# Reduced-precision passes for the ±1 convolutions, and expert rows scattered to token order

## The chip, the cores and the metric

The kernel runs on one core of a Trainium2 chip. A core has a matrix engine (TensorE, PE in the profile, with its weight loads as PEld), three engines for the rest (VectorE or DVE, ScalarE or ACT, GpSimd or POOL), a queue engine that mostly issues transfers (SyncE or SP), and 16 DMA engines that move data between the memory of the chip (DRAM tiles) and the core's own memory. Every engine works through its own list of instructions in order and waits on semaphores for the others. The metric is the device time of one execution in microseconds; runs of one kernel lie within some 0.2% of each other here.

## The reference, cut to what matters

The input `x` is (4, 256, 48, 48) in FP32: four images with 256 channels and 2304 tokens (pixels). Two layers follow each other; what is computed in FP32 there has to be met closely, because routing decisions hang on it.

- Layer 0: a 7x7 convolution with dilation 2 gives attention weights over 49 taps, and the attention is added to `x`. Then a router picks the 1151 tokens of each image with the largest weight, and these alone go through an FFN (256 to 1024 to 256).
- Layer 1, convolution: the normalised image is convolved with four kernels of 64 outputs each, two horizontal and two vertical of 5 taps, dilation 1 and 2. Their weights are binarised, `where(w < 0, -1, 1)`, so each product is the input or its negative. The four results side by side are again 256 channels and are added to `x`.
- Layer 1, experts: each token's norm is multiplied with gate weights for 8 experts; softmax gives a probability and the first expert with the largest one. Tokens take slots of their expert in token order, 1440 at most. Each expert is an FFN (256 to 1024 to 256, ReLU); its result is multiplied by the gate's probability, infinities and NaN are replaced, and it is added to the token's row. A token without a slot keeps its row.

The output is the image with channels in front.

## The kernel before, in words

*First stage (to about 2020 us).* Layer 0's convolution and attention, image by image. Beside it zeros are written into `xbuf`, the buffer of 11520 expert slots in DRAM, 40 writes of 292.5 KB on the SP queue, since slots that stay empty must hold numbers.

*Second stage (to 3020 us).* First seven FFNs of layer 0, on 384 rows each, beside the rank counts of the last image. Then a loop of 24 steps (`for s in ...`, from L640), one for each group of 384 tokens (8 image rows), with five more FFNs in every second of its first steps. It is a software pipeline written out by hand: what depends on other engines is issued a step later, so that five groups are under way at once. In one step stand, in this order of issue:
 - `load`: a group's rows from DRAM into `xt3`, a tile that keeps the residual stream of every token on the core to the end, and their channel norm. `token_norm` (L105 to L111) is statistics on VectorE (L107, L108), an addition and a power on GpSimd (L109, L110, tile `bnrs`), and the final scaling on VectorE (L111). It is called three times for a group.
 - `to_channels`: transposes on TensorE (`pn`, L511), and a copy of each half into the padded image `xq` (L513), one by ScalarE and one by VectorE.
 - `conv1`: 7 offsets x 2 halves of the channels x 2 (horizontal and vertical) = 28 FP32 products of 384 columns on shifted views of `xq` (L524, `pc`); the weights `cw` hold 1, -1, and 0 where one of a pair has no tap. ScalarE adds the bias into `cv` (L528).
 - `to_tokens`: transposes back (`pcv`, L539), the addition to the residual in `xt3` (L541), and the second norm into `row` (3 buffers), whose columns past the channels are set to zero by GpSimd (L535).
 - `gate`: transposes (`pl`), the gate product (`pgate`), softmax and choice of expert in a dozen small VectorE operations; the probability is put into `row` as column 256.
 - `place`: running counts give each token's slot; `gslot` and `kept` keep slot and mark for the end, `si` (L616) is the slot as an integer, too large for a token that finds no place. Three indirect writes from GpSimd (L618) scatter `row` (260 numbers a token) into `xbuf`. Writes to one DRAM tile wait for each other.

*Third stage (to 3701 us).* 24 passes, three for each expert, of 480 slots. `gather` (a plain read) brings the slots' rows as `xe` (three buffers), asked for a pass ahead; transposes; two products (`peh` L702, `pey` L710); VectorE adds a bias (L712), multiplies by the probability (L713) and repairs what isn't finite (L721 to L724); a plain write stores the result in `ybuf` (L725), by slot.

*Last stage (to 3814 us).* For each of the 72 tiles of 128 tokens GpSimd gathers the rows by slot (`yt`, L757), VectorE multiplies by `kept` and adds `xt3` (L760), TensorE transposes (`po`, L763), ScalarE and VectorE copy to `o`, and SP writes the output (L767).

Of the kernel before, what the change touches and what calls it, by code (L numbers as in the profile page):

```python
# [8 lines left out]
F32 = mybir.dt.float32  # L9
I32 = mybir.dt.int32  # L10
# [6 lines left out]
P = 128  # L17
B, C, H, W = 4, 256, 48, 48
HW = H * W  # 2304 tokens of an image
NT = HW // P  # 18 tiles of 128 tokens  # L20
NG = 6  # groups of 8 image rows
GT = 384  # tokens of a group
KA = 49  # attention taps
SELK = 1151  # tokens that layer 0's FFN processes: top_k's first k - 1
NSEL = 9  # tiles of 128 ranks that hold them
E, CAP = 8, 1440  # experts, and the slots of each
FF = 1024
NF = FF // P
XROW = 260  # a row of the experts' buffer: 256 channels, the gate, padding
HOFF = [-4, -2, -1, 0, 1, 2, 4]  # offsets of layer 1's convolutions  # L30
FMAX = 3.4028234663852886e38

# One image, by row and column parity, is four 24x24 images in which the 7x7
# convolution and the attention have no dilation. They are padded to 30x30.
SP = 30
SRC = 10 * SP  # source pixels of four output rows
PITCH = 306  # a row of the attention matrix in DRAM; skewed writes use PITCH + 1
# [3 lines left out]
def metaformer_kernel(ctx: ExitStack, tc: tile.TileContext, i, out):  # L41
# [18 lines left out]
    # before[p, j] = j < p; after[p, j] = j > p; upto[p, j] = p <= j  # L60
# [13 lines left out]
    # 1 for every rank but the last of the ninth tile  # L74
# [3 lines left out]
    ids = const.tile([P, NT], I32, tag="ids", name="ids")  # L78
    nc.gpsimd.iota(ids, pattern=[[P, NT]], base=0, channel_multiplier=1)

# [14 lines left out]
    # rows of layer 0: [x + LN(x) | LN(x)], by image  # L95
    xl = [dram.tile([HW, 2 * C], F32, tag=f"xl{b}", name=f"xl{b}") for b in range(B)]
    # token of each rank, by image
    order = [dram.tile([HW, 1], I32, tag=f"order{b}", name=f"order{b}") for b in range(B)]
    xbuf = dram.tile([E * CAP, XROW], F32, tag="xbuf", name="xbuf")
    ybuf = dram.tile([E * CAP, C], F32, tag="ybuf", name="ybuf")  # L100

    def token_norm(work, src, dst, eps, np_=P):
        """dst = LN(src) over the free dim of [np_, 256]."""
# [9 lines left out]
    # Ranks of an image's router weights, ties by the lower token, are counted three tiles at  # L113
    # a time beside the next image's convolution.
# [4 lines left out]
    # the first tile has no earlier tokens, the last no later ones  # L119
# [3 lines left out]
    def rank_rows(b, ps):  # L123
        """An image's router weights along the free dim of every partition."""
        w = w_img[b]
        nc.vector.tensor_scalar_add(w, w, br)
        for k0 in range(0, NT, 4):
            n = min(4, NT - k0)
            pt = ps.tile([P, 4, P], F32, tag="t", name=f"pw{b}_{k0}")
            for k in range(n):  # L130
                nc.tensor.transpose(
                    pt[:, k], w[:, k0 + k:k0 + k + 1].to_broadcast([P, P]), ident)
            nc.scalar.copy(wrow[:, k0 * P:(k0 + n) * P],
                           pt[:, :n].rearrange("p k t -> p (k t)"))

    def rank_count(b, j):
        """Tokens that come before each token of tiles 3j..3j+2."""
# [21 lines left out]
    # ======================================================================  # L159
    # Layer 0: dynamic 7x7 attention, and the ranks of its tokens  # L160
    # ======================================================================
    with ExitStack() as s1:
# [28 lines left out]
        # batch norm as k2 * inv + shift  # L191
# [12 lines left out]
        # normalised image, channels by parity image; its padding stays zero  # L204
        xp = wpool.tile([P, 2, 4, SP, SP], F32, tag="xp", name="xp")
        nc.vector.memset(xp.rearrange("p c q r x -> p (c q r x)"), 0.0)
        # the last six columns of each row of 30 stay zero
        k1s = [wpool.tile([P, 4, 4, SP], F32, tag=f"k1{n}", name=f"k1{n}") for n in range(2)]
        # attention rows spread over the sources' pitch; what is no tap stays zero
# [7 lines left out]
        # empty slots of the experts hold zeros  # L217
        zero = wpool.tile([P, 585], F32, tag="zero", name="zero")
        nc.gpsimd.memset(zero, 0.0)
        zrows = xbuf.rearrange("n r -> (n r)").rearrange("(k p r) -> k p r", p=P, r=585)  # L220
# [3 lines left out]
        def norm_a(b, j):  # L224
            """Subtract the channel means of 8 image rows; start the variance."""
# [32 lines left out]
        def conv(b, g):  # L258
            """Convolution of output rows 4g..4g+3 of the four parity images."""
# [11 lines left out]
        def sources(b, g):  # L271
            """Sources with pixels on partitions, four padded rows at a time."""
# [17 lines left out]
        def attend(b, g):  # L290
            """Softmax over the taps, laid out as a matrix [target, source]."""
# [27 lines left out]
        def mix(b, g):  # L319
            """x += attention; then tokens, their norm, and their router weights."""  # L320
# [40 lines left out]
        for s in range(B * NG + 1):  # L361
# [5 lines left out]
            # rows that the next image's group takes are no longer read  # L367
# [14 lines left out]
            for k in range(2 * s, min(2 * s + 2, 40)):  # L382
                nc.sync.dma_start(zrows[k], zero)

    # tokens of the residual stream from here to the end, by image
    xpool = pool("xtok", 1)
    xt3 = [xpool.tile([P, NT, C], F32, tag=f"xt3_{b}", name=f"xt3_{b}") for b in range(B)]
    gslot = [xpool.tile([P, NT], I32, tag=f"gslot{b}", name=f"gslot{b}") for b in range(B)]
    kept = [xpool.tile([P, NT], F32, tag=f"kept{b}", name=f"kept{b}") for b in range(B)]

    # ======================================================================
    # Layer 0's FFN on the selected tokens; layer 1's convolutions and routing
    # ======================================================================
    with ExitStack() as s2:
# [14 lines left out]
        # The horizontal pair, then the vertical: each is one convolution with 128 outputs  # L409
        # over the offsets of both, with zeros where one of them has no tap.  # L410
        cws = []
        for n in range(2):
            cw = wpool.tile([P, 2, 7, P], F32, tag=f"cw{n}", name=f"cw{n}")
            nc.gpsimd.memset(cw.rearrange("p c t o -> p (c t o)"), 0.0)
# [19 lines left out]
        # E - e, so that the first of equal experts is the largest  # L434
# [3 lines left out]
        # tokens that each expert has so far, in every partition  # L438
        taken = wpool.tile([P, E], F32, tag="taken", name="taken")
        nc.gpsimd.memset(taken, 0.0)  # L440
        # normalised image, padded by 4; its padding stays zero
        xq = wpool.tile([P, 2, H + 8, W + 8], F32, tag="xq", name="xq")
        nc.gpsimd.memset(xq.rearrange("p c r x -> p (c r x)"), 0.0)

        def fetch(b, h):
            """Rows of 384 ranks."""
# [12 lines left out]
        def ffn(b, h, idx2, g):  # L459
            """x + LN(x) + w * FFN(LN(x)), back to the tokens' rows."""  # L460
# [36 lines left out]
        def load(b, g):  # L497
            """8 rows of layer 1's input, and their channels' norm."""
            x = xt3[b][:, 3 * g:3 * g + 3]
# [5 lines left out]
            return xn  # L505

        def to_channels(b, g, xn):
            for cc in range(2):
                pt = ps_t.tile([P, GT], F32, tag="t", name=f"pn{b}_{g}_{cc}")
                for k in range(3):  # L510
                    nc.tensor.transpose(pt[:, k * P:(k + 1) * P],  # L511
                                        xn[:, k, cc * P:(cc + 1) * P], ident)
                (nc.vector.tensor_copy if cc else nc.scalar.copy)(  # L513
                    xq[:, cc, 4 + 8 * g:12 + 8 * g, 4:4 + W],
                    pt.rearrange("p (r x) -> p r x", x=W))

        def conv1(b, g):
            cv = work.tile([P, 2, GT], F32, tag="cv", name=f"cv{b}_{g}")
            for n in range(2):
                ps = ps_m.tile([P, GT], F32, tag="m", name=f"pc{b}_{g}_{n}")  # L520
                for t, d in enumerate(HOFF):
                    dy, dx = (d, 0) if n else (0, d)
                    for cc in range(2):
                        nc.tensor.matmul(  # L524
                            ps, lhsT=cws[n][:, cc, t],
                            rhs=xq[:, cc, 4 + 8 * g + dy:12 + 8 * g + dy, 4 + dx:4 + dx + W],
# [286 lines left out]
```

## Time and profile before

The time is 3820.05 us, the median of three runs (3817.47 to 3824.94). The profiled execution has a span of 3814.3 us.

| stage | from to (us) | span | TensorE busy |
|---|---|---|---|
| first two convolution steps | 2284.9 to 2323.2 | 38.3 | 37.9 |
| steps with five FFNs among them | 2323.2 to 2620.8 | 297.6 | 289.1 |
| thirteen plain steps | 2620.8 to 2955.6 | 334.8 | 325.4 |
| drain of the routing | 2955.6 to 3019.7 | 64.1 | 16.9 |
| experts | 3019.7 to 3700.7 | 681.0 | 668.4 |
| last stage | 3700.7 to 3814.3 | 113.6 | 50.8 |

Line numbers (L524) are those of the kernel printed above. In a line of groups the fields are: line, engine, operation, output<-inputs by the names of the tiles, shape, count (x), then busy microseconds, nanoseconds of one, and the idle time of the engine just before, with what ended it. An FP32 product leaves two weight loads and two matrix records. In a line of a stage the fields are the window, its length, the busy time of each engine in the order PE, PEld, DVE, ACT, POOL with the number of its records, then TensorE's granted clock as a share of the full one, the busy share of the DMA engines and the GB/s that they moved. In a line of waits the waiting engine, tile and line come first, then whom it waited for, then microseconds in total, number of times and the longest. A line of the timeline has start, duration, engine, line, operation and, in brackets, how long the engine was idle before it and what released it. Waits of an engine that is not the bottleneck cost nothing.

### The profile page before, as it was taken

How to read it: one execution, taken by the hardware profiler on the slowest of the kernel's cores; microseconds unless marked ns; L12 is line 12 of the kernel's file. 1: busy time of each engine (PE TensorE's matmuls, PEld its weight loads, DVE VectorE, ACT ScalarE, POOL GpSimd, SP SyncE). 2: the span in 40 equal slices, each digit the busy share in tenths (PEclk: the TensorE clock that was granted, in tenths of full speed). 3: DMA queues.
4: the chain of work that ended last, by engine and by line, in shares of the span. 5: the costliest groups of instructions: out<-in, count | busy, mean ns of one | idle time of the engine just before them, and what ended most of it. 6: DMA issues, size and time to landing. Idle time of an engine off the chain costs nothing. (4 is left out here: it accounts for less than half of the span.)

```text
span 3814.3 us, 32485 instructions
## 1 busy us (share of the span) xinstructions
PE 3545.5 (93%) x12832; PEld 2248.8 (59%) x12832; DVE 1211.3 (32%) x3618; ACT 434.0 (11%) x779; POOL 480.0 (13%) x774
## 2 busy tenths in 40 slices
PE   6999999999999999999994789999999499999985
PEld 3566666666666666666663556666565366666652
DVE  3012124312235112261116312333443243333434
ACT  1001000000100000100001111211010022121211
POOL 1000001100001000020002322232332100000006
PEclk9999999999999999999996889999999699999995
DMA  7001100001100000110002221111000222222106
GB/s 231 13 25 39 36 25 25 25 25 35 40 25 25 25 25 27 34 27 21 21 21 76 62 63 31 41 34 44 18 17 18 80 61 59 59 62 66 49 27 193
DMA packets 122840, 174.36 MB, mean 46 GB/s; under 512 B 17089, under 2 KB 96193, under 8 KB 122689
## 3 DMA queue, kind: packets, MB, share of 16 engines
q1 hardware_dynamic: 92800, 111.41, 10.4%
q0 software_dynamic: 13824, 33.23, 2.9%
q10 hardware_dynamic: 16064, 27.66, 2.2%
q8 instruction: 100, 1.64, 0.2%
q14 instruction: 52, 0.42, 0.0%
HBM read 91.69 MB, written 80.58 MB: 45 GB/s over the span
## 5 line engine op out<-in xcount | busy, mean ns | idle before, releaser
L264 PE MATMUL c<-xp,cw 128*128 128x384 f32 x4704 | 1568.5, 492 | 0.9 <-DVE xp L256 0.9
L264 PEld LDWEIGHTS c<-xp,cw 128*128 128x128 f32 x4704 | 885.0, 189 | 663.0 <-issue 304.1
L524 PE MATMUL pc<-xq,cw 128*128 128x384 f32 x1344 | 467.1, 501 | 0.0
L329 DVE COPY av<-pa 120x192 f32<-120x192 f32 x96 | 32.0, 358 | 1096.9 <-PE pa L327 1096.9
L524 PEld LDWEIGHTS pc<-xq,cw 128*128 128x128 f32 x1344 | 254.8, 195 | 164.6 <-issue 12.8
L710 PE MATMUL pey<-ew,ehid 128*120 128x256 f32 x1536 | 335.4, 379 | 0.0
L702 PE MATMUL peh<-xeT,ew 128*128 128x480 f32 x768 | 316.5, 571 | 3.1 <-ACT xeT L697 3.1
L710 PEld LDWEIGHTS pey<-ew,ehid 128*120 128x120 f32 x1536 | 281.1, 183 | 59.2 <-issue 10.4
L109 POOL TENSOR_SCALAR bnrs<-bnmv 128x1 f32<-128x1 f32 x216 | 47.1, 223 | 1865.3 <-DVE bnmv L108 1864.0
L702 PEld LDWEIGHTS peh<-xeT,ew 128*128 128x128 f32 x768 | 145.0, 191 | 159.7 <-issue 151.0
L337 PE MATMUL pv<-av,xt 120*128 120x96 f32 (+1 forms) x1152 | 226.6, 329 | 0.0
L337 PEld LDWEIGHTS pv<-av,xt 120*128 120x128 f32 (+1 forms) x1152 | 181.8, 214 | 39.3 <-issue 11.4
L712 DVE TENSOR_TENSOR ey<-pey,eb 120x256 f32<-120x256 f32 x96 | 40.7, 424 | 431.1 <-PE pey L710 431.1
L269 ACT ACTIVATE k<-c,cb 128x384 f32<-128x384 f32 x24 | 14.0, 583 | 1323.4 <-PE c L264 1266.1
L757 POOL DMA_INDIRECT yt<-ybuf,gslot x72 | 69.9, 971 | 720.8 <-DMA ybuf<-ey 699.1
L704 ACT ACTIVATE ehid<-peh,eb 128x480 f32<-128x480 f32 x192 | 127.0, 662 | 294.6 <-PE peh L702 293.2
L480 PE MATMUL ph<-gt,fw 128*128 128x384 f32 x384 | 137.8, 520 | 6.2 <-ACT gt L475 5.8
L486 PE MATMUL py<-fw,hid 128*128 128x256 f32 x576 | 126.8, 379 | 3.0 <-DVE y L489 3.0
L110 POOL TENSOR_TENSOR bnrs<-bnrs,mhalf 128x1 f32<-128x1 f32 x216 | 125.0, 583 | 13.3
L486 PEld LDWEIGHTS py<-fw,hid 128*128 128x128 f32 x576 | 109.3, 190 | 21.1 <-DVE y L489 3.8
L480 PEld LDWEIGHTS ph<-gt,fw 128*128 128x128 f32 x384 | 76.7, 203 | 63.6 <-ACT gt L475 9.5
L763 PE MATMUL po<-ident,yt 128*128 128x128 f32 x144 | 50.8, 448 | 57.2 <-DVE yt L760 56.1
(169 smaller groups left out, 2599.3 us busy)
## 6 DMA issues: line engine op xcount, KB each, us to landing
xl<-rows SPq DMA_DIRECT2D x24, 768.0 KB, 3.5
ew<-in_L_ffn_w_dram ACTq DMA_DIRECT2D x16, 1024.0 KB, 5.4
skew<-sp SPq DMA_DIRECT2D x24, 575.6 KB, 4.3
at<-skew SPq DMA_DIRECT2D x24, 562.5 KB, 4.8
xbuf<-zero SPq DMA_DIRECT2D x40, 292.5 KB, 7.8
xe<-xbuf SPq DMA_DIRECT2D x24, 487.5 KB, 4.5
ybuf<-ey SPq DMA_DIRECT2D x24, 480.0 KB, 3.6
x<-in_x_dram SPq DMA_DIRECT2D x24, 384.0 KB, 3.4
```

The source lines that it names most:

```text
L109: nc.gpsimd.tensor_scalar_add(rs[:np_], mv[:np_, 1:2], eps)
L110: nc.gpsimd.tensor_tensor(rs[:np_], rs[:np_], mhalf[:np_, 0:1], ALU.pow)
L264: nc.tensor.matmul(ps, lhsT=cw1[:, cc, t, :], rhs=xp[:, cc, :, 4 * g + ki:4 * g + ki + 4, kj:kj + 24], start=(t == 0 and cc == 0), stop=(t ...
L337: nc.tensor.matmul(pv[:, q], lhsT=xts[b, g + k][:n, q, cc * P:(cc + 1) * P], rhs=av[:n, q, k], start=(k == 0), stop=(k == 2))
L480: nc.tensor.matmul(ph, lhsT=fw1[:, cc, f * P:(f + 1) * P], rhs=gt[:, cc], start=(cc == 0), stop=(cc == 1))
L486: nc.tensor.matmul(py, lhsT=hid[:, f, k * P:(k + 1) * P], rhs=fw2[:, f], start=(f == 0), stop=(f == NF - 1))
L524: nc.tensor.matmul(ps, lhsT=cws[n][:, cc, t], rhs=xq[:, cc, 4 + 8 * g + dy:12 + 8 * g + dy, 4 + dx:4 + dx + W], start=(t == 0 and cc == 0) ...
L702: nc.tensor.matmul(ph, lhsT=w1[:, cc, f * P:(f + 1) * P], rhs=xeT[:, cc], start=(cc == 0), stop=(cc == 1))
L704: nc.scalar.activation(hid[:, f], ph, AF.Relu, bias=eb1[:, e * NF + f:e * NF + f + 1])
L710: nc.tensor.matmul(py[:R], lhsT=hid[:, f, j * R:(j + 1) * R], rhs=w2[:, f], start=(f == 0), stop=(f == NF - 1))
L757: nc.gpsimd.indirect_dma_start(out=y, out_offset=None, in_=ybuf, in_offset=bass.IndirectOffsetOnAxis(ap=gslot[b][:, n:n + 1], axis=0))
L763: nc.tensor.transpose(pts[cc][:, k * P:(k + 1) * P], y[:, cc * P:(cc + 1) * P], ident)
```

## The change

*Convolution.* Weights and image become F32R, a type of four bytes that TensorE multiplies with reduced precision instead of as full FP32. So that nothing is lost, the image is kept as two parts: ScalarE's copy into the F32R tile rounds it to its leading bits (`hi`), and VectorE subtracts that from the original (`lo`). [...]the products of both parts are added in the same accumulator. A step has 56 F32R products in place of 28 FP32 ones.

*Rows.* A row of `xbuf` grows from 260 to 516 numbers: 256 channels of the norm, the probability, the token's number, padding, and the residual (256). `to_tokens` writes the residual into the row instead of into a resident tile, and also, by a plain write on SP, into `fin`, a DRAM tile in token order. Zero rows carry a token number past the end. In the experts, VectorE adds the residual to the result, and GpSimd scatters the rows into `fin` by their token numbers, four indirect writes of 120 rows a pass; empty slots are skipped by the bounds check. `ybuf`, `xt3`, `gslot` and `kept` go. The last stage reads `fin` with 24 plain loads of 384 KB on ScalarE's queue, transposes and stores.

The core of the diff:

```diff
-XROW = 260  # a row of the experts' buffer: 256 channels, the gate, padding
+XHEAD = 260
+XROW = XHEAD + C
+NONE = 1 << 30
...
-    ybuf = dram.tile([E * CAP, C], F32, tag="ybuf", name="ybuf")
+    fin = dram.tile([B * HW, C], F32, tag="fin", name="fin")
...
-        zero = wpool.tile([P, 585], F32, tag="zero", name="zero")
-        nc.gpsimd.memset(zero, 0.0)
-        zrows = xbuf.rearrange("n r -> (n r)").rearrange("(k p r) -> k p r", p=P, r=585)
+        zero = wpool.tile([P, 2, XROW], F32, tag="zero", name="zero")
+        nc.gpsimd.memset(zero.rearrange("p j r -> p (j r)"), 0.0)
+        nc.gpsimd.memset(zero[:, :, C + 1:C + 2].bitcast(I32), NONE)
+        zrows = xbuf.rearrange("(k p j) r -> k p j r", p=P, j=2)
...
-            for k in range(2 * s, min(2 * s + 2, 40)):
+            for k in range(2 * s, min(2 * s + 2, 45)):
                 nc.sync.dma_start(zrows[k], zero)
...
-            cw = wpool.tile([P, 2, 7, P], F32, tag=f"cw{n}", name=f"cw{n}")
+            cw = wpool.tile([P, 2, 7, P], F32R, tag=f"cw{n}", name=f"cw{n}")
...
-        xq = wpool.tile([P, 2, H + 8, W + 8], F32, tag="xq", name="xq")
+        xqs = []
+        for part in ("hi", "lo"):
+            xq = wpool.tile([P, 2, H + 8, W + 8], F32R, tag=f"xq{part}", name=f"xq{part}")
...
-                (nc.vector.tensor_copy if cc else nc.scalar.copy)(
-                    xq[:, cc, 4 + 8 * g:12 + 8 * g, 4:4 + W],
-                    pt.rearrange("p (r x) -> p r x", x=W))
+                hi, lo = (xq[:, cc, 4 + 8 * g:12 + 8 * g, 4:4 + W] for xq in xqs)
+                full = pt.rearrange("p (r x) -> p r x", x=W)
+                nc.scalar.copy(hi, full)
+                nc.vector.tensor_sub(lo, full, hi.bitcast(F32))
...
                     for cc in range(2):
-                        nc.tensor.matmul(
-                            ps, lhsT=cws[n][:, cc, t],
-                            rhs=xq[:, cc, 4 + 8 * g + dy:12 + 8 * g + dy, 4 + dx:4 + dx + W],
-                            start=(t == 0 and cc == 0), stop=(t == 6 and cc == 1))
+                        for xq in xqs:
+                            nc.tensor.matmul(
+                                ps, lhsT=cws[n][:, cc, t],
+                                rhs=xq[:, cc, 4 + 8 * g + dy:12 + 8 * g + dy,
+                                       4 + dx:4 + dx + W],
+                                start=(t == 0 and cc == 0 and xq is xqs[0]),
+                                stop=(t == 6 and cc == 1 and xq is xqs[1]))
...
-            nc.gpsimd.memset(row[:, :, C + 1:], 0.0)
+            nc.gpsimd.memset(row[:, :, C + 2:XHEAD], 0.0)
+            nc.gpsimd.tensor_copy(
+                row[:, :, C + 1].bitcast(I32), ids[:, b * NT + 3 * g:b * NT + 3 * g + 3])
...
-                nc.vector.tensor_add(x[:, k], pt, x[:, k])
-                token_norm(work, x[:, k], row[:, k, :C], 1e-5)
+                xk = row[:, k, XHEAD:]
+                nc.vector.tensor_add(xk, pt, x[:, k])
+                token_norm(work, xk, row[:, k, :C], 1e-5)
+            n0 = b * HW + g * GT
+            nc.sync.dma_start(fin[n0:n0 + GT, :].rearrange("(k p) c -> p k c", p=P),
+                              row[:, :, XHEAD:])
...
-            nc.sync.dma_start(ybuf[n0:n0 + N, :].rearrange("(j p) c -> p j c", p=R), y)
+            for j in range(J):
+                nc.vector.tensor_add(y[:, j], y[:, j], xe[:, j, XHEAD:])
+                nc.gpsimd.indirect_dma_start(
+                    out=fin,
+                    out_offset=bass.IndirectOffsetOnAxis(
+                        ap=xe[:, j, C + 1:C + 2].bitcast(I32), axis=0),
+                    in_=y[:, j], in_offset=None, bounds_check=B * HW - 1, oob_is_err=False)
...
-                for k in range(3):
-                    n = 3 * g + k
-                    y = work.tile([P, C], F32, tag="y", name=f"yt{b}_{n}", bufs=8)
-                    nc.gpsimd.indirect_dma_start(
-                        out=y, out_offset=None, in_=ybuf,
-                        in_offset=bass.IndirectOffsetOnAxis(ap=gslot[b][:, n:n + 1], axis=0))
-                    nc.vector.scalar_tensor_tensor(y, y, kept[b][:, n:n + 1], xt3[b][:, n],
-                                                   ALU.mult, ALU.add)
...
+                y = work.tile([P, 3, C], F32, tag="y", name=f"yt{b}_{g}", bufs=8)
+                nc.scalar.dma_start(y, fin[n0:n0 + GT, :].rearrange("(k p) c -> p k c", p=P))
+                o = work.tile([P, 2, GT], F32, tag="o", name=f"o{b}_{g}", bufs=3)
```

## The prediction

> **What bounds the kernel now.** I read the busy table and its slices first, then the costliest groups, then the windows of the stages that the change touches, then the waits and the timeline of single steps.
>
> ```profile
> PE 3545.5 (93%) x12832; PEld 2248.8 (59%) x12832; DVE 1211.3 (32%) x3618; ACT 434.0 (11%) x779; POOL 480.0 (13%) x774
> L524 PE MATMUL pc<-xq,cw 128*128 128x384 f32 x1344 | 467.1, 501 | 0.0
> L757 POOL DMA_INDIRECT yt<-ybuf,gslot x72 | 69.9, 971 | 720.8 <-DMA ybuf<-ey 699.1
> ```
>
> TensorE is busy for 93% of the span. The convolution of layer 1 (L524) shows 1344 records for 672 products. The last 72 gathers start only when the experts are done. By stage (span, then busy time of each engine, granted clock, DMA share):
>
> ```profile
> 2284.90:2323.20 38.30, 37.91 (x128) 22.48 (x126) 4.57 (x16) 3.54 (x7) 4.11 (x5) 1.00 0.10 28
> 2323.20:2620.80 297.60, 289.06 (x1118) 191.14 (x1119) 97.31 (x436) 52.93 (x90) 82.63 (x146) 0.98 0.11 33
> 2620.80:2955.60 334.80, 325.42 (x1255) 201.22 (x1254) 140.93 (x711) 33.05 (x69) 106.72 (x213) 0.97 0.07 25
> 2955.60:3019.70 64.10, 16.93 (x84) 14.18 (x82) 20.68 (x130) 2.69 (x7) 16.64 (x25) 0.56 0.34 107
> 3019.70:3700.70 681.00, 668.44 (x2496) 447.97 (x2496) 240.26 (x353) 140.46 (x216) 0.00 (x0) 0.99 0.20 53
> 3700.70:3814.30 113.60, 50.84 (x144) 23.92 (x144) 52.15 (x104) 11.50 (x24) 69.92 (x72) 0.51 0.56 171
> ```
>
> Rows 1 to 3 are the 24 convolution steps, row 1 the first two, row 2 those with five FFNs among them, row 3 thirteen plain ones. Row 4 drains the routing, row 5 is the 24 expert passes, row 6 the last stage. In rows 1 to 3 TensorE is busy for 97% and more, so it sets the pace there; in row 6 it is not.
>
> TensorE is only just the bound of a plain step. In row 3 a step lasts (2955.6-2645.6)/13 = 23.85 us by the first `pcv` transpose of each step. GpSimd's waits in that row, and a step's timeline on it:
>
> ```profile
> POOL bnrs L109 <- DVE bnmv L108: 76.7, 72, 5.0
> POOL xbuf L618 <- DVE si L616: 54.5, 13, 5.9
> POOL xbuf L618 <- DMA xbuf<-row,si: 52.5, 28, 2.3
> POOL row L535 <- DMA xbuf<-row,si: 22.3, 13, 2.0
> 2764.15 0.11 POOL L535 MEMSET row<- 128x9 f32 x1 [1.79 <-DMA xbuf<-row,si]
> 2767.29 0.22 POOL L109 TENSOR_SCALAR bnrs<-bnmv 128x1 f32<-128x1 f32 x1 [3.04 <-DVE bnmv L108]
> 2780.29 1.09 POOL L618 DMA_INDIRECT xbuf<-row,si  x1 [3.88 <-DVE si L616]
> 2783.41 0.97 POOL L618 DMA_INDIRECT xbuf<-row,si  x1 [2.02 <-DMA xbuf<-row,si]
> 2786.19 0.98 POOL L618 DMA_INDIRECT xbuf<-row,si  x1 [1.82 <-DMA xbuf<-row,si]
> 2788.85 0.11 POOL L535 MEMSET row<- 128x9 f32 x1 [1.67 <-PE pc L524]
> ```
>
> From 2767.3 to 2788.8 GpSimd goes through a chain: six norms at 1.5 us, each passed to VectorE and back, then VectorE's small gate operations at 0.2 us each until `si`, then three scatters, each held until the one before has landed, 2.8 to 3.1 us apart. That is 21.5 us of dependent work in a step of 23.3 to 24 us, although GpSimd counts as busy for 32% of it.
>
> **What the Trainium skill says.** "FP8 and Floating Point Precision", TensorE Precision Notes: true FP32 takes four passes, the reduced form reads 4-byte FP32 and truncates it. The trace agrees on the four: 48 records of `pc` took 15.79 us, so a product (two records) takes 0.65 us, four times 0.163. "TensorE: Matmul & The Clock Gate", Back-to-back issue gap: N/2.4 + 2.5 ns, an estimate of 0.163 us for 384 columns. No run here shows a reduced pass yet. Same page, LDWEIGHTS: columns/1.2, an estimate of 0.107 us for 128; the trace agrees, ten gate products with 8 columns came 0.113 us apart, weights included. So the load can hide under 0.163. "DMA: Bandwidth & Descriptors", Anatomy of one DMA (SWDGE): 2.0 us + bytes/436e3 for a GpSimd DMA; the trace's scatter has a median of 2.6 us to landing where this gives an estimate of 2.3 for 133 KB. I use only its slope.
>
> **The change, part by part.**
>
> *Convolution.* 28 FP32 products of a step (28 x 0.65 = 18.4 us) become 56 reduced ones, each a single pass over 384 columns: 56 x 0.163 = 9.2 us. Saved on TensorE: 9.2 us a step, 221 us over 24. The bounds of the unknown price are one pass (0.163) and four (0.65); I take one. The rest of TensorE's step stays (transposes, gate: about 4.9 us), so its plain step would be 14.2 us.
>
> *What the step then runs into.* The GpSimd chain is not shortened by the same amount. As built, the order on GpSimd alternates between two kinds of step. In one the three scatters stand in a row behind `si`: from the memset to the first scatter the timeline has 16.1 us, of which I take off 1.8, the part of the 3.0 us ahead of the first norm in which TensorE's transposes are awaited; with the scatters' 3 x 3.15 = 9.5 that is 23.8. In the other the scatters lie between the norms: 1.3 to the first norm, norms 9.1, two scatters' issue at 1.0, the last scatter 3.15, sum 15.5. Two steps are 39.3 us, 19.6 a step. The scatter goes from 2.85 to 3.15 us since a row has 2064 bytes instead of 1040 (+131 KB/436e3 = 0.3). VectorE gains a 0.53 us subtraction per half and loses two small operations, ScalarE gains one copy of 0.48; neither is full (VectorE 141 of 335 us). So plain steps give 23.85-19.6 = 4.2 us each, 55 us over thirteen. Bounds: 0 (chain not compressible at all, 23.85) and 9.2 (TensorE still the bound).
>
> *Steps with an FFN.* Two steps and an FFN now take (2620.8-2344.0)/4 = 69.2 us. TensorE's minimum becomes 2 x 14.2 + 20.8 (the FFN's own records in the timeline) = 49.2; chain and FFN one after the other would be 39.3 + 20.8 = 60.1; I take the middle, 54.6. That saves 14.6 x 4 = 58, and with 9 for the odd step in row 2, 67 us. In row 1 the 112 records save at most 112 x 0.163 = 18; I take 15, as the chain is only filling. Sum of the three: 137 us.
>
> *Waits that the wider row brings.* The residual now lies in `row`, so the addition at L541 cannot start before the three scatters and the new 384 KB write of three steps back are done. Behind it on VectorE stand all norms and gates. Scatters of step s end about a step before row s+3 is first written, so I cost it at nothing, hidden by that step; the bound is one scatter, 3 us a step, which the 23.85 end holds.
>
> *Start and drain.* Zero rows are 45 x 528 KB instead of 40 x 292.5 KB, on a queue idle beside the PE-bound first stage; I take +2 for the start (0 to 5), where 231 GB/s are in use. In the drain twelve scatters follow one another: 12 x 0.3 = +4. The first expert load is twice as large: +1.
>
> *Experts.* 24 times four additions of 0.42 us (the same shape at L712) and four scatters. VectorE is busy 10 of 28.4 us in a pass, GpSimd for none; four chained scatters are about 12 us. The `xe` buffer is held by 7 + 12 us more into the next pass, but with three buffers it is wanted only a pass later. TensorE's 668 of 681 us hide all: 0.
>
> *Last stage.* Before: experts end at 3700.7, the NaN repair at 3708.0, the write to `ybuf` lands, the first gather is issued at 3712.4, and then 72 gathers at 1.25 us (0.95 and 0.30 to issue) are 90 us; the output ends at 3814.3. After:
>
> ```profile
> 3706.63 1.35 DVE L724 COPY_PREDICATED_SCALAR ey<-ad_AluOpType.not_equal,none 120x1024 f32 x1
> 3712.41 0.99 POOL L757 DMA_INDIRECT yt<-ybuf,gslot  x1 [699.06 <-DMA ybuf<-ey]
> 3713.70 0.97 POOL L757 DMA_INDIRECT yt<-ybuf,gslot  x1 [0.30 <-issue]
> ```
>
> repair at 3708, first addition 0.5, four chained scatters 4 x 2.9 = 11.6, so the first plain load goes out at 3720 and lands at 3723. Then 9.44 MB in and 9.44 MB out. The last stage moved 171 GB/s at a DMA share of 0.56, an estimate of 305 GB/s at full share: 62 us. TensorE (51 us at half clock), VectorE and ScalarE fit under that. With 3 us for the last output the end is 3788: 26 us gained. Bounds: 0 (loads and stores hinder each other, 215 GB/s) and 33 (343 GB/s, the output queue's bytes by its own packets' time in that row).
>
> Sum: 3820 - 137 + 2 + 4 + 1 - 26 = **3664**.
>
> **Rivals.** (1) *TensorE stays the bound*: the chain compresses, since much of it is waiting for transposes that now come earlier (5.0 and 5.9 us longest waits for VectorE). Against it: the scatters' 9 us and norms' 9 us are latencies that no faster TensorE shortens. Time: 3820-221-26+7 = 3580. (2) *A reduced pass costs two column times* (0.326), so that 56 of them equal 28 FP32 products: nothing saved in the convolutions, only the end: 3820-26+7 = 3801. For it: each FP32 record in the trace is 0.326 long, so that a pass of one has not been seen; against it: the weight load is shorter than 0.163 and no step of the product asks for two passes. (3) *Slower*: a reduced product takes as long as an FP32 one, 0.65. Then convolutions double: 3820+443-26+7 = 4244. Only the record of four passes for full FP32 speaks against it, and the name of the type. A milder way to the slower side is that waits for `row` and chained scatters lengthen steps to more than 25 us and the experts' scatters hold back `xe`; that needs some 35 us over the gain at the end and no gain from conv, and VectorE's and GpSimd's slack speaks against it.
>
> **How the numbers follow.** Chain-bound 0.62 (3664); TensorE-bound 0.18 (3580); two column times 0.12 (3801); slower 0.08. The predicted time is the first case's. The range reaches from 3560, a little below rival 1, to 3745: all 13 plain steps unchanged (+55) and the end without gain (+26). It leaves out rivals 2 and 3, 0.20. Rival 2 is still faster by 0.5%, so faster has 0.90, same 0.02, slower 0.08.
>
> **What would show it right or wrong.** `pc` again 1344 records, now 0.163 us apart instead of 0.326: right on the price; 0.326 or more: rival 2 or 3. Plain steps about 19.6 us apart, TensorE below 80% busy there, and GpSimd waiting for `si` and for its own scatters: the chain. Steps of 14 to 15 us: rival 1. Expert passes still at 28.4 us; longer ones, with `xe` waited for, would refute the hidden scatters. Last stage 88 us or so with the DMA share at 0.9 after the first load. What I trust least is the chain's 19.6 us, put together from pieces of a step in which TensorE set the pace.

## The result, and the profile after

The changed kernel takes 3657.27 us, the median of four runs (3644.95 to 3666.56); the kernel before 3822.49 us in the same comparison. The ratio is 0.956, with a 95% interval of 0.954 to 0.959. The profiled execution has a span of 3651.0 us, 163.3 less than before. The runs measure time; how many bits the two parts of the image keep, none of them shows.

The page's busy table of the changed kernel, and three groups of it:

```profile
PE 3354.9 (92%) x12832; PEld 2263.0 (62%) x12832; DVE 1224.9 (34%) x3618; ACT 444.1 (12%) x803; POOL 522.5 (14%) x824
L532 PE MATMUL pc<-xqhi,cw 128*128 128x384 f32 x672 | 248.6, 370 | 0.0
L532 PE MATMUL pc<-xqlo,cw 128*128 128x384 f32 x672 | 243.5, 362 | 0.0
L740 POOL DMA_INDIRECT fin<-ey,xe x96 | 101.9, 1061 | 615.2 <-DVE ey L739 433.0
```

TensorE's busy share hardly moved, 93 to 92%, although its time fell by 191 us. The convolution still has 1344 records, now 672 on each part of the image. (Their busy time overlaps, so it must not be read as the price of a product; that comes from the distance of their starts.) The 96 scatters from the experts are new.

The price of a product: the first and the last of the first 56 in the changed kernel and what starts behind them, then the first 56 records (28 products) of the kernel before and what starts behind those.

```profile
2273.31 0.42 PE L532 MATMUL pc<-xqhi,cw 128*128 128x384 f32 x1
...
2283.33 0.34 PE L532 MATMUL pc<-xqlo,cw 128*128 128x384 f32 x1
2283.51 0.71 PE L517 MATMUL pn<-ident,xn 128*128 128x128 f32 x5
2285.04 18.31 PE L524 MATMUL pc<-xq,cw 128*128 128x384 f32 x56
2303.18 0.82 PE L511 MATMUL pn<-ident,xn 128*128 128x128 f32 x6
```

The 56 reduced products take 10.2 us from the first start to the next instruction, 0.182 each at a granted clock of 1.00; the 28 FP32 products take 18.1, 0.65 each. So a step saves 8.0 us on TensorE.

The same stages as before, in the same columns (window, length, PE, PEld, DVE, ACT, POOL, granted clock, DMA share, GB/s):

```profile
2273.30:2294.30 21.00, 21.00 (x122) 20.92 (x121) 5.07 (x17) 3.31 (x7) 4.30 (x5) 1.00 0.19 51
2294.30:2551.50 257.20, 234.01 (x1126) 194.99 (x1125) 101.54 (x432) 57.64 (x100) 84.14 (x152) 0.93 0.20 63
2551.50:2805.30 253.80, 227.74 (x1256) 215.79 (x1254) 146.66 (x695) 38.73 (x82) 107.03 (x222) 0.89 0.24 82
2805.30:2882.70 77.40, 19.29 (x83) 14.42 (x82) 21.44 (x123) 2.68 (x7) 19.82 (x32) 0.53 0.41 133
2882.70:3571.40 688.70, 669.42 (x2496) 448.44 (x2496) 273.37 (x446) 140.06 (x216) 97.64 (x92) 0.99 0.27 66
3571.40:3651.00 79.60, 32.44 (x144) 26.44 (x144) 21.80 (x35) 11.48 (x24) 4.24 (x4) 0.58 0.71 240
```

Row by row against before: first two steps 38.3 to 21.0, steps with FFNs 297.6 to 257.2, thirteen plain steps 334.8 to 253.8, together 139 us less; drain 64.1 to 77.4, 13 more; experts 681.0 to 688.7, 8 more; last stage 113.6 to 79.6, 34 less. The loop also begins 11.6 us earlier (2273.3 against 2284.9). The sum is the 163 us.

In the plain steps TensorE is now at 90% of the time at a granted clock of 0.89, so it waits there, which it did not before. The waits of the changed kernel from 2577 to 2767, ten plain steps, and the first additions into the row in three of them:

```profile
POOL bnrs L115 <- DVE bnmv L114: 32.4, 31, 3.2
POOL xbuf L631 <- DMA xbuf<-row,si: 24.3, 12, 2.6
DVE row L553 <- DMA xbuf<-row,si: 18.4, 6, 3.8
POOL xbuf L631 <- DVE si L629: 9.7, 5, 2.3
2653.03 0.76 DVE L553 TENSOR_TENSOR row<-pcv,x 128x256 f32<-128x256 f32 x2 [2.63 <-DMA xbuf<-row,si]
2669.66 0.73 DVE L553 TENSOR_TENSOR row<-pcv,x 128x256 f32<-128x256 f32 x2
2691.50 0.76 DVE L553 TENSOR_TENSOR row<-pcv,x 128x256 f32<-128x256 f32 x2 [3.10 <-DMA xbuf<-row,si]
```

The third line is new. Before, the same addition waited for TensorE's transposes (ten plain steps, from 2646 to 2884):

```profile
DVE xt L541 <- PE pcv L539: 104.0, 11, 10.7
```

Now VectorE stands still in every second step until the scatters of an older row have landed. The start times of the additions also give the step: 15 to 17 and 22 to 23 us in turn, 18.9 on average over ten (2577.4 to 2766.6), where it was 23.8. In the last stage the loads and stores fill the DMA engines (from 3595 to 3645):

```profile
3595.00:3645.00 50.00, 30.68 (x138) 25.05 (x137) 12.28 (x23) 11.00 (x23) 0.00 (x0) 0.60 1.01 340
```

### The profile page after: what moved, and what is told of

Same layout as the page of the kernel before. It is cut to its first block, busy times and chain, and to the rows that moved or that the text cites. A ratio compares the mean times of both kernels' runs of the same rounds, so it can differ in the third digit from the quotient of the medians.

```text
span 3651.0 us, 32778 instructions
## 1 busy us (share of the span) xinstructions
PE 3354.9 (92%) x12832; PEld 2263.0 (62%) x12832; DVE 1224.9 (34%) x3618; ACT 444.1 (12%) x803; POOL 522.5 (14%) x824
## 5 line engine op out<-in xcount | busy, mean ns | idle before, releaser
L532 PE MATMUL pc<-xqhi,cw 128*128 128x384 f32 x672 | 248.6, 370 | 0.0
L532 PE MATMUL pc<-xqlo,cw 128*128 128x384 f32 x672 | 243.5, 362 | 0.0
L740 POOL DMA_INDIRECT fin<-ey,xe x96 | 101.9, 1061 | 615.2 <-DVE ey L739 433.0
L486 PE MATMUL ph<-gt,fw 128*128 128x384 f32 x384 | 145.3, 539 | 14.1 <-DVE gt L481 10.1
L532 PEld LDWEIGHTS pc<-xqhi,cw 128*128 128x128 f32 x672 | 137.8, 205 | 0.1
L532 PEld LDWEIGHTS pc<-xqlo,cw 128*128 128x128 f32 x672 | 136.8, 204 | 0.5 <-DVE xqlo L522 0.3
```

The source lines that it names most:

```text
L486: nc.tensor.matmul(ph, lhsT=fw1[:, cc, f * P:(f + 1) * P], rhs=gt[:, cc], start=(cc == 0), stop=(cc == 1))
L532: nc.tensor.matmul(ps, lhsT=cws[n][:, cc, t], rhs=xq[:, cc, 4 + 8 * g + dy:12 + 8 * g + dy, 4 + dx:4 + dx + W], start=(t == 0 and cc == 0 ...
L740: nc.gpsimd.indirect_dma_start(out=fin, out_offset=bass.IndirectOffsetOnAxis(ap=xe[:, j, C + 1:C + 2].bitcast(I32), axis=0), in_=y[:, j], ...
```

## The experiments

All were compared with the kernel before on the same chip as they ran. The table gives the median, the ratio with its interval, and from each trace the loop (first to last convolution product), the mean of ten plain steps (first addition to first addition; the ten don't begin at the same step in every row, which moves the mean by up to 0.5), the drain (last convolution product to first expert transpose), and the experts (first transpose to last product), in us. A trace is one execution, and executions of one kernel lay up to 0.8% apart here (3565 to 3594 us for the shared norm with five row buffers), more than the 0.2% given above.

| kernel | time | ratio to before | loop | step | drain | experts |
|---|---|---|---|---|---|---|
| before | 3822 | 1 | 670.6 | 23.8 | 64.1 | 680 |
| changed | 3657 | 0.956 (0.954 to 0.959) | 531.6 | 18.9 | 77.8 | 688 |
| rows only, FP32 | 3784 | 0.990 (0.987 to 0.992) | 676.2 | 24.0 | 75.1 | 684 |
| passes only | 3627 | 0.948 (0.946 to 0.951) | 479.8 | 16.0 | 65.2 | 679 |
| changed, high part only | 3620 | 0.946 (0.944 to 0.949) | 486.7 | 19.5 | 93.7 | 687 |
| 5 row buffers | 3609 | 0.944 (0.942 to 0.947) | 500.1 | 16.9 | 72.3 | 682 |
| 4 row buffers | 3611 | 0.948 (0.945 to 0.950) | 502.9 | 17.0 | 73.2 | 687 |
| 5 row buffers, high part only | 3560 | 0.933 (0.930 to 0.935) | 434.7 | 14.8 | 80.8 | 689 |
| free scatters | 3614 | 0.947 (0.944 to 0.950) | 514.3 | 18.0 | 59.7 | 686 |
| shared norm | 3623 | 0.948 (0.945 to 0.951) | 503.2 | 17.7 | 75.8 | 687 |
| shared norm, 5 row buffers | 3574 | 0.935 (0.932 to 0.938) | 466.8 | 15.1 | 76.6 | 686 |
| the same, 5 expert buffers | 3581 | 0.938 (0.935 to 0.940) | 466.3 | 15.0 | 76.8 | 681 |
| rows only, FP32, 5 row buffers | 3790 | 0.994 (0.992 to 0.996) | 670.6 | 23.8 | 75.1 | 684 |

(With the high part only and three row buffers, three additions of the loop come after its last product, where the changed kernel has two; so more of the pipeline falls into its drain, 93.7 us.)

**The two halves of the change, each alone.** Rows only: one image tile in FP32 and 28 products, all else as changed.

```diff
-        for part in ("hi", "lo"):
-            xq = wpool.tile([P, 2, H + 8, W + 8], F32R, tag=f"xq{part}", name=f"xq{part}")
+        for part in ("hi",):
+            xq = wpool.tile([P, 2, H + 8, W + 8], F32, tag=f"xq{part}", name=f"xq{part}")
```

> The changed kernel with its convolutions put back to FP32 (one image tile, 28 products a step); rows, scatter to token order and last stage stay changed. If the two parts add up as by the stages (convolution loop -139 us, last stage -34, drain +13, experts +8, start -12), this keeps only the second kind: about 3820-34+8+8 = 3800 us, or 3790 if the 12 us at the start belong to it too; the loop from the first to the last convolution product at 671 us as before. Rival: the wider row and the wait for its buffer cost much in the loop and the passes hide it; then the FP32 loop is longer than 671 us and the time above 3820.

Passes only, on the kernel before. Both passes read the one tile with the leading bits, and the small part goes into a scratch tile:

```diff
-                        nc.tensor.matmul(
-                            ps, lhsT=cws[n][:, cc, t],
-                            rhs=xq[:, cc, 4 + 8 * g + dy:12 + 8 * g + dy, 4 + dx:4 + dx + W],
-                            start=(t == 0 and cc == 0), stop=(t == 6 and cc == 1))
+                        for part in range(2):
+                            nc.tensor.matmul(
+                                ps, lhsT=cws[n][:, cc, t],
+                                rhs=xq[:, cc, 4 + 8 * g + dy:12 + 8 * g + dy,
+                                       4 + dx:4 + dx + W],
+                                start=(t == 0 and cc == 0 and part == 0),
+                                stop=(t == 6 and cc == 1 and part == 1))
```

> The kernel before with F32R convolutions, 56 products a step; both passes read the tile with the leading bits, [...]so the small parts are left out of the sum (they are computed, into a scratch tile). Timing of the passes is that of the change. If the loop is bound by the chain of scatters and norms and not by the wait for the row buffer: loop near 535 us, last stage still 113 us, drain 64, so about 3680 us. If the wider row and its wait cost the loop something: shorter than 532, down to 500, time near 3650. Rival, a loop of 671 us less 24 x 8.4 = 470 us: TensorE would be the bound here, about 3620 us.

Measured: rows alone save 34 us, passes alone 191, the sum 225, but the change as a whole 165. The halves get in each other's way by some 60 us, and most of it is in the loop. With the old rows it falls by 190.8 us to 479.8, and a step to 16.0; that is 24 times the 8.0 us that a step saves on TensorE. With the new rows it falls only to 531.6, and a step to 18.9. In FP32 the same new rows cost the loop 5.6 us, and the time of rows only came out 6 to 16 us below what I had expected. My expectation for passes only was a loop near 535, or down to 500 if the wider row mattered; it went below even that. The ten plain steps of passes only, in a window and in their waits:

```profile
2586.40:2746.40 160.00, 145.02 (x902) 141.98 (x900) 103.68 (x532) 28.81 (x62) 79.94 (x160) 0.97 0.07 26
```

```profile
DVE row L112 <- DMA xbuf<-row,si: 22.4, 10, 3.3
POOL xbuf L624 <- DMA xbuf<-row,si: 20.3, 10, 2.8
```

The three scatters and six norms are all there, in 16.0 us. So the chain on GpSimd, which the prediction put at 19.6 us, isn't that long. (As a kernel this half is of no use, since the small part is missing from the sum. A second image tile would take 25 KB of each partition, beside 72 KB of `xt3`, by their shapes; no run tried it.) A wait for the row's scatters is there too, 22.4 us, but it stands at the scaling of the norm (L112), behind the additions and the statistics. As the loop fell by all that the products save, it can have cost little; a run of this kernel with more row buffers was not made.

**Is TensorE the bound of the changed loop?** The products of the small part are left out.

```diff
-                        for xq in xqs:
+                        for xq in xqs[:1]:
```

> The changed kernel without the products of the small part: 28 F32R products a step, everything else (subtraction included) as in the change; the convolution's low bits are left out. If the plain steps are bound by the chain on GpSimd and VectorE, the pair of steps stays near 37.8 us and the time falls by little, 0 to 40 us (FFN steps and the first steps, where TensorE is busier). If TensorE is the bound: 28 x 0.18 = 5 us a step, 121 us over 24, about 3536 us.

The plain step did not fall (19.5 against 18.9 us); TensorE isn't its bound. Pairs of steps with an FFN fell from 58.8 to 50.2 us (mean of four), so there it is still on the path. The test is not quite clean, as TensorE with less to do ran at a mean granted clock of 0.68 in ten plain steps. The wait of VectorE for the row took more:

```profile
DVE row L553 <- DMA xbuf<-row,si: 31.3, 5, 6.5
PE pcv L550 <- DVE row L553: 29.5, 5, 7.0
```

Five times in ten steps it waited 6 us, and TensorE's transposes waited behind it.

**Taking the row's wait away.** More buffers make the addition wait for older rows.

```diff
-            row = work.tile([P, 3, XROW], F32, tag="row", name=f"row{b}_{g}", bufs=3)
+            row = work.tile([P, 3, XROW], F32, tag="row", name=f"row{b}_{g}", bufs=5)
```

> The changed kernel with five row buffers in place of three. The addition into the row then waits for scatters of five steps back, not three. If that wait (2.5 to 3.8 us in every second plain step) lies on the path: pairs shorter by 3 us or more, 35 us over the loop, 3620 us. If GpSimd's own chain of scatters and norms is the bound and the wait only mirrors it: pairs stay at 37 to 38 us, the time within 10 us of 3657.

> The changed kernel with four row buffers. A row lives from the first addition until its third scatter has landed, some 60 us in the steps that wait; with three buffers that allows a step each 20 us, with four each 15. If the row's life sets the step, four buffers already give what five gave: loop 498 to 510 us, time near 3610. If it is only a matter of the order in which VectorE is given its work, between 3610 and 3657 with waits for the scatters left at the addition.

> FP32 convolutions with the wide rows and five row buffers: a control. TensorE needs 23.3 us a step there, longer than a third of the row's life, so more buffers should give nothing in the loop (670 to 676 us; 3784 with three buffers, within 8 us). If five buffers gained 30 us or more here too, the wait would not belong to the shorter step.

Five buffers save 48 us by the medians, 31.5 of them in the loop; four save about the same (their intervals overlap). In ten plain steps of the kernel with five, the addition at L553 waits only for transposes:

```profile
POOL xbuf L631 <- DVE si L629: 37.8, 10, 3.9
POOL xbuf L631 <- DMA xbuf<-row,si: 37.4, 20, 4.3
DVE row L553 <- PE pcv L550: 11.7, 7, 3.2
POOL bnrs L115 <- DVE bnmv L114: 7.2, 10, 0.7
```

GpSimd now waits longer for its own scatters and for `si` than in the changed kernel, and the kernel is faster: those waits were not the bound. The control agrees. With FP32 products, which make the step 24 us, VectorE waited for rows too (rows only, from 2622 to 2960):

```profile
DVE row L552 <- DMA xbuf<-row,si: 40.1, 4, 10.2
```

Yet five buffers took only 5.6 us off that loop, and the time stayed within what such runs differ by (3784 and 3790).

So three rows are too few for the short step. A row is taken by the first addition and given back when the third scatter has landed, two steps of the pipeline later. The row taken at 2593.0 was waited for at 2653.0: 60 us, in which no more than three groups can start, and VectorE, which does all the rest in order, stands still meanwhile.

This life isn't a constant: two whole steps are in it, so it shrinks with them. I count it to 3.0 us after the issue of the third scatter, the median landing. In ten plain steps of the changed kernel a row lived 54.6 us on average (45 to 52 and 56 to 61 in turn); a third of that is 18.2, beside a step of 18.9. With five buffers it lived 60.1 us at a step of 16.9, so that 3.6 rows were in use at a time, and four buffers are enough. The write of the residual to `fin` doesn't hold the row: in the five steps for which the trace has its landing, it came 4.9 to 6.1 us after the first addition.

**What the life of a row is made of.** Free scatters: the three scatters of a group go to three buffers and don't wait for each other. The experts read the first buffer alone, so two thirds of the tokens miss their expert.

```diff
-                    out=xbuf,
+                    out=xbufs[k],
```

> Three row buffers as in the change, but the three scatters of a group go to three DRAM buffers, of which the experts read only the first: two thirds of the tokens reach no expert (they keep their residual row). The scatters of a group no longer wait for each other, so the row is free some 6 us earlier. If the row wait is the length of the scatters' chain: loop as with five buffers or shorter, 490 to 505 us, and the drain 77 - 8 x 2.2 = 60 us or less; time 3657 - 35 - 17 = 3605. If the wait is for the write of the residual or for VectorE's own order: loop at 530, only the drain shorter, 3640.

Shared norm: statistics of the three tiles, then one addition and one power on GpSimd for all three.

```diff
+        nc.gpsimd.tensor_scalar_add(rs, mv[:, :, 1], eps)
+        nc.gpsimd.tensor_tensor(rs, rs, mhalf[:, 0:3], ALU.pow)
+        for k, (src, dst) in enumerate(zip(srcs, dsts)):
+            nc.vector.tensor_scalar(dst, src, mv[:, k, 0:1], rs[:, k:k + 1],
+                                    ALU.subtract, ALU.mult)
```

> The shared norm with the change's three row buffers. If the row wait holds the step (theory after the first runs), norms hardly matter: loop 515 to 532 us, time 3640 to 3657. If the prediction's chain of norms and scatters does: four crossings less at 1.5 us are 6 us a step, loop 450 us or TensorE's 475, time near 3600.

With three buffers, free scatters shorten the loop by 17 us and a step by 0.9, the shared norm by 28 us and 1.2. Both are part of a row's life and both shorten it (52.7 and 51.4 us, against 54.6), but neither ends the wait. In ten plain steps of each, free scatters first:

```profile
DVE row L554 <- DMA xbuf<-row,si: 21.2, 11, 2.4
DVE row L565 <- DMA xbuf<-row,si: 17.0, 6, 3.2
```

Each fell beside what I had expected: I had taken scatters for the whole of the wait and norms for nothing. The drain, where no products hide anything, gains 18 us from free scatters.

**What bounds the loop once the wait is gone.**

> Five row buffers, and the products of the small part left out (28 F32R products a step; the convolution's low bits are missing). With three row buffers leaving them out left the plain steps as they were. If five buffers have made TensorE the bound, each step falls by 28 x 0.18 = 5 us: plain steps from 16.9 to about 12, loop from 500 to 380 us, time near 3490. If the chain of VectorE and GpSimd is the bound behind the row wait too, only the FFN pairs fall (10 us each, 50 together): loop 450, time near 3560.

> Five row buffers, and the norms of a group's three tiles share one addition and one power on GpSimd (shape 128x3) instead of three pairs of 128x1: four of six crossings between VectorE and GpSimd a step are gone. If these crossings (1.5 us each) hold the step: plain steps from 16.9 to 15, TensorE's own 15.1; loop 475 us, time near 3585. If TensorE or the scatters hold it: loop 495 to 505, time within 8 us of 3609. Longer, if the scaling of a tile now waits for the statistics of all three.

With five buffers, leaving out the small part does shorten plain steps, from 16.9 to 14.8 us, but not by the 5 us of the products. Whether 14.8 is the chain's own length, or that of a TensorE that ran at a mean granted clock of 0.79 there (2539 to 2686), no run separates; in either case the chain that I had put at 19.6 fits into 14.8. With five buffers and the shared norm a step takes 15.1 us at a granted clock of 1.00:

```profile
2575.80:2726.70 150.90, 143.00 (x902) 136.99 (x901) 99.72 (x510) 28.24 (x61) 59.25 (x91) 1.00 0.31 103
```

TensorE is busy for 95% of it, and the longest waits of ScalarE are for its products; by these signs the loop of 467 us is the first one with both halves of the change that TensorE bounds again. (The trace is that of the slowest of four executions, 3594 us.) At 3574 us this version is faster than the kernel before, and than the changed one by some 2%.

**The experts' extra 8 us.** Five buffers for `xe`, on the last version.

```diff
-            xe = work.tile([R, J, XROW], F32, tag="xe", name=f"xe{e}_{q}", bufs=3)
+            xe = work.tile([R, J, XROW], F32, tag="xe", name=f"xe{e}_{q}", bufs=5)
```

> Five row buffers, the shared norm, and five buffers for the expert rows instead of three. With five, an expert row load no longer waits until the scatters of a pass three back have read it. If the seven waits of TensorE for these loads (9 us in the version with three) come from that, experts take 680 instead of 686 us and the time is near 3568; if the load's length of 7.2 us and the order in which transposes are issued make them, experts stay at 686 and the time at 3574.

With three buffers TensorE waited five times for expert rows after the first pass (from 2850 to 3560):

```profile
PE pe L721 <- DMA xe<-xbuf: 9.0, 5, 2.6
```

With five buffers there is no such wait in that stretch, and the stage fell from 686.0 to 680.7 us, that of the kernel before. So the buffer, held by the scatters into the next pass, made the waits. What they cost is less certain: with three such buffers the stage takes anything from 682 to 689 us in the table. The whole time doesn't show it (3581 and 3574 overlap in their runs): the kernels differ by more at the start. In the traces of the kernels with the changed rows, layer 1's first convolution product came between 2262 and 2287 us, although little but the norms of two groups differs up to there.

## Why the prediction was right, and where it was not

The time was forecast at 3664 and came at 3657, and the loop's gain at 137 us where 139 were measured. The agreement is better than the reasons: the plain step came out at 18.9 us, close to the 19.6 forecast, but something else holds it there, and that is luck. Outside the loop drain and experts cost 16 us more than forecast, start and last stage 22 us less, and that cancelled too.

- *Price of a pass.* Right in kind: one pass each, nothing of rivals 2 and 3. A reduced product took 0.182 us at full clock, not 0.163, and a step's 28 FP32 products cost 18.1, so 8.0 us are saved and not 9.2. The estimate after the Trainium skill ("TensorE: Matmul & The Clock Gate", Back-to-back issue gap) was a tenth low here, and the measured number stands. The prediction's agreement on four passes rested on that estimate; by the measured price an FP32 product costs 3.6 reduced ones.
- *What the step runs into.* Right that TensorE stops being the bound, wrong in what takes its place. The prediction's step "As built, the order on GpSimd alternates ... 19.6 a step" added norms and scatters to a chain that would bound any fast kernel. Passes only ran the same chain in 16.0 us, and with five row buffers and few products it fitted into 14.8. Adding up a step in which everybody waited for TensorE's transposes counted waits as work. One of its own signs said so: TensorE was busy for 90% of the plain steps, not for less than 80.
- *Waits that the wider row brings.* This is the step that failed outright: "I cost it at nothing, hidden by that step". The wait was named, its place at the front of VectorE's step too, and with 3 us a step as bound. It is what sets the pace: 31.5 us of the loop come back with two more buffers, and 52 separate the loop from that of passes only. It was hidden while a step took 23.8 us, and the same edit called for a step shorter than a third of the row's life.
- *Split of the loop.* Plain steps saved 81 us (55 forecast), the first two and the FFN steps 58 (82 forecast). A pair with an FFN took 58.8 us, not the middle of 54.6 but nearly the upper end of 60.1, where chain and FFN follow one another. These two errors cancelled.
- *Drain.* +5 forecast, +14 measured. The scatter's median landing went from 2.6 to 3.0 us, 0.4 where 0.3 was worked out, and twelve make 5 us; the expert load landed in 7.2 instead of 4.5, 2.7 us; and the last row's addition waited 6.7 us for scatters, the same overlooked wait (with five row buffers the drain is 5.5 us shorter).
- *Experts.* 0 forecast, +8 measured: 3 us while TensorE waits for the second, larger load at the start, the rest, by the last experiment, from the `xe` buffers that scatters hold. The step "with three buffers it is wanted only a pass later" overlooked that the first half of the next pass's transposes is issued ahead of a pass's products.
- *Last stage.* 26 forecast, 34 measured. The scatter chain came as forecast (first load at 3591.4, 20.0 us into the stage; 19.3 forecast). The transfers ran faster than the 305 GB/s worked out: 340 at full share.
- *Start.* +2 forecast, 12 us earlier measured; this lies within the spread between kernels noted above and I have no cause for it. (The zero rows are 45 x 516 KB in the unit of the 292.5 KB, not 528.)

Rival 1 (TensorE stays the bound, 3580) got 0.18. Passes only bear its mechanism out: there the loop fell by all that TensorE saves. With the new rows its time was reached only with five row buffers and the shared norm together (3574); the row buffers alone gave 3609.

## What to carry to other kernels

When a bound engine is sped up, check each rotating buffer. The time from the first write to the last landed read, divided by the number of buffers, is a floor for the step. Where the life has whole steps in it, as here, measure it again at the new step. And the floor alone doesn't say what more buffers are worth: with FP32 products a row lived 71 us at a step of 24.0, so three rows were in use there as well, and five buffers gained next to nothing.

It matters, too, who has to wait. Before, a wait for old rows stood at a memset on GpSimd; after, it stood at an addition at the front of VectorE's step, with all other work of VectorE behind it.

Last, two halves of a change are worth running apart: here the passes alone ran faster than both halves together.

## What the runs showed of the hardware

TensorE pays twice for waits. Six lines of its timeline in a plain step of the changed kernel (start, duration, and in brackets the wait before):

```profile
2655.03 0.34 PE L532 MATMUL pc<-xqhi,cw 128*128 128x384 f32 x1
2655.22 0.34 PE L532 MATMUL pc<-xqlo,cw 128*128 128x384 f32 x1
...
2661.15 0.66 PE L574 MATMUL pl<-ident,row 128*128 128x128 f32 x4 [2.79 <-DVE row L117]
...
2663.60 0.48 PE L517 MATMUL pn<-ident,xn 128*128 128x128 f32 x1 [0.95 <-DVE xn L117]
...
2668.47 0.52 PE L532 MATMUL pc<-xqlo,cw 128*128 128x384 f32 x1
2668.79 0.52 PE L532 MATMUL pc<-xqhi,cw 128*128 128x384 f32 x1
```

Before the waits products start 0.18 us apart, after them 0.32; the granted clock from 2665 to 2670 was 0.50. The Trainium skill describes this ("TensorE: Matmul & The Clock Gate", Part 1: The HAM clock gate: half the clock after an idle window of some 3.4 us, and about as long until the full one is back). The trace agrees on the half, though the longer of the two waits was 2.8 us; back at 0.18 was TensorE at 2670.5, some 7 us after the second wait, longer than that figure, with many small products between. The mean granted clock over ten plain steps was 0.98 before, 0.86 after the change, 0.94 with five row buffers and 1.00 with the shared norm besides. So part of what a wait costs the loop is this slow restart; how much of the 31.5 us, no run separates.
